# A two-layer convolution kernel on one core: kernel table by complex products, `u` stored from GpSimd, a variance product between the halves of an encoding

## The chip, the cores and the metric

The kernel runs on one core of a Trainium2 chip. The metric is the device time of one execution in microseconds (us). Three runs of the kernel before took 12704.01, 12707.76 and 12716.35 us, with the median 12707.76 us. One further execution was taken with the hardware profiler; every duration below is from that one.

Engines are named as the profile names them: PE is TensorE (matmuls; PEld is its weight loads), DVE is VectorE, ACT is ScalarE, POOL is GpSimd and SP is SyncE, which here only issues transfers. A name with a q (SPq, ACTq) is an engine's issue of a transfer.

## What is computed

The input `x` has 32 images of 128 channels by 32 x 32 pixels, in float32. Two layers run one after the other, each added to its input; the change touches only the beginning of the first:

```python
x = x + _L0_conv_ref(_gn(x), ...)     # group norm, then the layer below

h = jnp.einsum('bdl,de->ble', u, W_enc) + b_enc      # u: [32, 128, 1024], 1024 outputs
dtA = A * dt[:, None]                                # A: [1024, 4], complex
Bd = (jnp.exp(dtA) - 1.0) / A
vand = jnp.exp(dtA[:, :, None] * t)                  # t = 0 .. 63
K = 2.0 * jnp.einsum('dn,dnl->dl', Cc * Bd, vand).real   # a causal filter of 64 taps per output
y = irfft(rfft(z) * rfft(K))[..., :L]                # z = h transposed: each row filtered with K
y = gelu(y + D[:, None] * z);  g = y @ W_glu + b_glu
...                                                  # gate, layer norm, decoding
# second layer: group norm, then a deformable convolution of 64 taps
```

The group norm `_gn` has 32 groups of 4 channels; it subtracts the mean of a group and divides by the square root of its variance.

## The kernel before

The program has four parts in a row: `ssm_kernel_table` (L42), `ssm_convolution` (L186), `main_block` (L590) and `deformable_redo` (L1342). The first runs beside the beginning of the second.

**The table.** `ssm_kernel_table` makes the 64 filter taps of all 1024 outputs. The outputs lie on 128 partitions by 8 chunks, with 4 complex modes each, so `KN` is 32. From the small [128, 32] arrays `re`, `im` (the real and imaginary part of dtA), `cbr` and `cbi` (of 2 C B) it makes [128, 32, 64] arrays: `e` = exp(re t) (L142, L143), the angle im t (L144), its sine and its cosine less one (`sincos`, L64 to L78: six DVE operations, two sines on ACT, one more on DVE), and then (cos cbr - sin cbi) e (L146 to L149). The sum over the 4 modes goes into `kp` (L155 to L158), and SP stores `kp` to `kp_d` (L159). A scheduler orders these operations among the first ones of the next part.

**The first encoding.** `ssm_convolution` goes through 8 chunks of 128 outputs: `encode(k)` and then `convolve(k, z)`. For k > 0, `encode` loads the normalised images `u` from `u_d` and multiplies them. For k = 0 it makes them: a loop over t = 0 .. 34 (L264) in which several images are under way, each by a generator `group_norm_steps` (L162) of five steps:

1. L169, ACT: copy of `xt` into `u` with the sum per channel;
2. L172, PE: the product with `gavg`, which gives the group mean;
3. L174 and L175, ACT: the negative mean, and the sum of squares about it (the elementwise result goes to `u` and is overwritten later);
4. L178, PE: the product for the variance;
5. L180 on ACT (square root), L181 and L182 on DVE (reciprocal, and `u` = (xt - mean) / deviation).

Iteration t does, in the order of the program: step 5 of image t-2; the store of that `u` to `u_d`, issued by ACT (L267); step 3 of image t-1; the load of `xt` of image t, issued by SP (L272), and step 1 of it; `image(t-3)`; step 4 of image t-1; step 2 of image t. `image(b, u)` (L232) multiplies the eight 128-pixel blocks of `u` with the encoding weights, four into each of two PSUM banks (L237, eight matmuls that the profile shows as 16 passes), and then two DVE operations (L242) add the bias and write `z[0]` and `z[1]`. This order is kept on every engine (`manual_schedule`), and each engine takes its own instructions strictly one after the other.

Buffers: `u` has 5, `xt` has 6 (tag `yo`), the small group norm values have 4. PSUM has 4 buffers of two banks, which the two small products of an image and its encoding take in turn. `z[1]` lies where the table's arrays were, and its first write waits for the store of `kp`.

**What follows.** `convolve` loads filter matrices `toe` from `kp_d` (SP, L302), multiplies (L320), and stores `y_d` from POOL (L357). `main_block` takes the bulk of the time. The change does not alter these parts.

Of the kernel before, what the change touches and what calls it, by code (L numbers as in the profile page):

```python
# [8 lines left out]
F32 = mybir.dt.float32  # L9
AF = mybir.ActivationFunctionType  # L10
ALU = mybir.AluOpType
# [4 lines left out]
P = 128  # L16
# [5 lines left out]
NT = 64  # L22
# [19 lines left out]
def ssm_kernel_table(nc, tc, ins, kp_d):  # L42

    KN = KD * N2
    with tc.tile_pool(name="ssm", bufs=1) as sp:
# [6 lines left out]
        def small(tag, shape=(P, KN)):  # L52
            return sp.tile(list(shape), F32, tag=tag, name=tag)
# [7 lines left out]
        tt = sp.tile([P, NT], F32, tag="tt", name="tt")  # L61
        nc.sync.dma_start(tt, ins["steps"].to_broadcast([P, NT]))

        def sincos(theta, shape, tag):  # L64

            k = small(f"{tag}_k", shape)
            r = small(f"{tag}_r", shape)
            nc.vector.tensor_scalar(k, theta, INV_2PI, MAGIC, op0=ALU.mult, op1=ALU.add)
            nc.vector.tensor_scalar(k, k, MAGIC, None, op0=ALU.subtract)
            nc.vector.scalar_tensor_tensor(r, k, -PI2_A, theta, op0=ALU.mult, op1=ALU.add)  # L70
            nc.vector.scalar_tensor_tensor(r, k, -PI2_B, r, op0=ALU.mult, op1=ALU.add)
            nc.vector.scalar_tensor_tensor(r, k, -PI2_C, r, op0=ALU.mult, op1=ALU.add)
            nc.vector.tensor_scalar(r, r, PI_MAX, -PI_MAX, op0=ALU.min, op1=ALU.max)
            s = small(f"{tag}_s", shape)
            nc.scalar.activation(s, r, AF.Sin)
            nc.scalar.activation(k, r, AF.Sin, scale=0.5)
            nc.vector.scalar_tensor_tensor(r, k, -2.0, k, op0=ALU.mult, op1=ALU.mult)
            return s, r  # L78
# [45 lines left out]
        cbr, cbi = small("cbr"), small("cbi")  # L124
# [7 lines left out]
        nc.vector.tensor_scalar_mul(cbi, cbi, 2.0)  # L132


        big = (P, KN, NT)
        e, ang = small("e", big), small("ang", big)
        t_b = tt[:, None, :].to_broadcast([P, KN, NT])

        def over_t(a):
            return a[:, :, None].to_broadcast([P, KN, NT])  # L140

        nc.vector.tensor_mul(e, over_t(re), t_b)  # L142
        nc.scalar.activation(e, e, AF.Exp)  # L143
        nc.vector.tensor_mul(ang, over_t(im), t_b)  # L144
        sv, cv = sincos(ang, big, "v")
        nc.vector.scalar_tensor_tensor(cv, cv, 1.0, over_t(cbr), op0=ALU.add, op1=ALU.mult)  # L146
        nc.vector.tensor_mul(sv, sv, over_t(cbi))
        nc.vector.tensor_sub(cv, cv, sv)
        nc.vector.tensor_mul(cv, cv, e)  # L149

        kp = sp.tile([P, KD, KPW], F32, tag="kp", name="kp")
        nc.gpsimd.memset(kp, 0.0)
# [9 lines left out]
def group_norm_steps(nc, pool, pm, gavg, eps, xt, out):  # L162


    s = pool.tile([P, 1], F32, tag="gn_s", name="gn_s")
    nm = pool.tile([P, 1], F32, tag="gn_m", name="gn_m")
    ss = pool.tile([P, 1], F32, tag="gn_ss", name="gn_ss")
    r = pool.tile([P, 1], F32, tag="gn_r", name="gn_r")
    nc.scalar.activation(out, xt, AF.Identity, accum_out=s)  # L169
    yield  # L170
    p = pm(0)
    nc.tensor.matmul(p, gavg, s, start=True, stop=True)  # L172
    yield
    nc.scalar.mul(nm, p, -1.0)  # L174
    nc.scalar.activation(out, xt, AF.Square, bias=nm, accum_out=ss)  # L175
    yield
    p = pm(1)
    nc.tensor.matmul(p, gavg, ss, start=True, stop=True)  # L178
    yield
    nc.scalar.activation(r, p, AF.Sqrt, bias=eps)  # L180
    nc.vector.reciprocal(r, r)  # L181
    nc.vector.tensor_scalar(out, xt, nm, r, op0=ALU.add, op1=ALU.mult)  # L182
    yield


def ssm_convolution(nc, tc, const, ins, x, u_d, kp_d, y_d):  # L186
# [12 lines left out]
    with tc.tile_pool(name="cvt", bufs=3) as tp, tc.tile_pool(  # L199
        name="cvz", bufs=1  # L200
    ) as zp, tc.tile_pool(name="cv1", bufs=1) as one, tc.tile_pool(
        name="cvu", bufs=5
    ) as up, tc.tile_pool(name="cvy", bufs=6) as yp, tc.tile_pool(
        name="cvg", bufs=4
    ) as gp, tc.tile_pool(name="cv_ps", bufs=4, space=PSUM) as psum:

        def banks(name):
            return psum.tile([P, 2, 512], F32, tag="ps", name=name)
# [11 lines left out]
        def block(g, j):  # L220

            return 2 * ORDER[j] + g

        def encode(k):

            z = [
                pool.tile([P, P // 2, NB, B, 2], F32, tag=f"z{g}", name=f"z_{k}_{g}")
                for g, pool in enumerate((one, zp))
            ]
            bias = b_enc[:, k * P : (k + 1) * P]  # L230

            def image(b, u):  # L232
                both = banks(f"psz_{k}_{b}").rearrange("p g (j d) -> p g j d", j=NB)
                for g in range(2):
                    for j in range(NB):
                        lo = block(g, j) * P
                        nc.tensor.matmul(  # L237
                            both[:, g, j, :], u[:, lo : lo + P], w_enc[:, k * P : (k + 1) * P],
                            start=True, stop=True,
                        )  # L240
                for g in range(2):
                    nc.vector.tensor_add(  # L242
                        z[g][:, :, :, b, :].rearrange("p d j e -> p j d e"),
                        both[:, g].rearrange("p j (d e) -> p j d e", e=2),
                        bias.rearrange("p (d e) -> p d e", e=2)[:, None].to_broadcast(
                            [P, NB, P // 2, 2]
                        ),
                    )

            if k > 0:  # L250
                for b in range(B):
                    u = up.tile([P, L], F32, tag="u", name=f"u_{k}_{b}")
                    nc.sync.dma_start(u, u_d[b])
                    image(b, u)
                return z


            running = {}

            def step(b):  # L260
                if b in running:
                    next(running[b][1])

            for t in range(B + 3):  # L264
                step(t - 2)
                if t - 2 in running:
                    nc.scalar.dma_start(u_d[t - 2], running[t - 2][0])  # L267
                step(t - 1)
                if t < B:
                    u = up.tile([P, L], F32, tag="u", name=f"u_{k}_{t}")  # L270
                    xt = yp.tile([P, L], F32, tag="yo", name=f"xt_{t}")
                    nc.sync.dma_start(xt, x[t])  # L272

                    def pm(n, t=t):
                        return banks(f"gn_ps_{t}_{n}")[:, 0, 0:1]

                    running[t] = u, group_norm_steps(
                        nc, gp, pm, const["gavg"], const["eps"], xt, u
                    )
                    step(t)  # L280
                if t >= 3:
                    image(t - 3, running.pop(t - 3)[0])
                step(t - 1)
                step(t)
            return z

# [82 lines left out]
        with tc.manual_schedule():  # L369
            for k in range(KD):  # L370
                convolve(k, encode(k))
# [1002 lines left out]
@with_exitstack  # L1374
def kernel(ctx: ExitStack, tc: tile.TileContext, ins, out):
    nc = tc.nc
    x = ins["x"]
    cpool = ctx.enter_context(tc.tile_pool(name="const", bufs=1))
    dram = ctx.enter_context(tc.tile_pool(name="scratch", bufs=1, space=DRAM))

    const = {}
    for name in ("gavg", "davg"):
        const[name] = cpool.tile([P, P], F32, tag=name, name=name)
        nc.sync.dma_start(const[name], ins[name])
    const["eps"] = cpool.tile([P, 1], F32, tag="eps", name="eps")
    nc.vector.memset(const["eps"], 1e-5)
    const["one"] = cpool.tile([P, 1], F32, tag="one", name="one")
    nc.vector.memset(const["one"], 1.0)
    offmax = cpool.tile([P, B], F32, tag="offmax", name="offmax")

    kp_d = dram.tile([D, KPW], F32, tag="kp_d", name="kp_d")
    u_d = dram.tile([B, C, L], F32, tag="u_d", name="u_d")
    y_d = dram.tile([D, B, NJ, P], F32, tag="y_d", name="y_d")
    x1_d = dram.tile([B, C, L], F32, tag="x1_d", name="x1_d")

    ssm_kernel_table(nc, tc, ins, kp_d)
    ssm_convolution(nc, tc, const, ins, x, u_d, kp_d, y_d)
    main_block(nc, tc, const, ins, x, u_d, y_d, x1_d, out, offmax)
    deformable_redo(nc, tc, const, ins, x1_d, out, offmax)
# [85 lines left out]
```

## Time and profile before

| | |
|---|---|
| median of three runs | 12707.76 us |
| the profiled execution, its own time | 12713.35 us |
| its span, from the first to the last instruction | 12711.4 us |
| mean granted PE clock | 0.973 |
| busy: PE, DVE, ACT, POOL | 96%, 61%, 43%, 71% of the span |
| 60 to 180 us (most of the first encoding): granted PE clock | 0.77 |
| the same stretch: PE, DVE, ACT, POOL busy | 92.2, 60.3, 68.8, 0 us of 120 |
| the same stretch: DMA share, and bytes moved | 0.67, 225 GB/s |
| first matmul of `convolve(0)` (L320) | at 181.48 us |

A row of the timeline reads: start and duration in us, engine, line, operation, result <- operands, sizes, count, and in brackets how long the engine had been idle and what ended that. In a table of stretches the columns are the stretch, its length, the busy time (and number) of PE, PEld, DVE, ACT and POOL, the granted PE clock as a share of full speed, the busy share of the DMA engines, and GB/s. In a list of waits they are the total in us, the number of times and the longest.

### The profile page before, as it was taken

To read this page: it belongs to the slowest core of one execution; us is meant where nothing else is said; L and a number is where in the kernel's file an instruction comes from. 1 tells how busy PE (TensorE), PEld (TensorE's weight loads), DVE (VectorE), ACT (ScalarE), POOL (GpSimd) and SP (SyncE) were. 2 spreads that over 40 slices of the span, in tenths; PEclk is the share of its full clock that TensorE was granted. 3 is DMA by queue.
4 is the path that set the end of the run, shared out by engine and by line. 5 is a ranking of instruction groups with operands and counts; after the bars stand their busy time and mean duration, and the time that the engine had idled before them with its cause. 6 is when DMAs were issued, how large, how long until landed. Compare 5 with 4: busy or idle time off the path is not lost.

```text
span 12711.4 us, 162031 instructions
## 1 busy us (share of the span) xinstructions
PE 12198.8 (96%) x51362; PEld 6670.1 (52%) x51362; DVE 7803.7 (61%) x14315; ACT 5485.8 (43%) x7823; POOL 8975.3 (71%) x11691
## 2 busy tenths in 40 slices
PE   7999899999999999999999999999999999999965
PEld 7999444444444444444444444444444444444444
DVE  5555126666666666666666666666666666666666
ACT  4344124444444444444444444444444444444443
POOL 2455127777777777777777777777777777777779
PEclk9999999999999999999999999999999999999976
DMA  7899236666766666667666676666666667667666
GB/s 237 266 277 277 74 82 181 180 183 186 188 179 179 177 177 188 181 177 186 179 185 180 185 188 180 178 176 177 188 180 182 184 179 186 181 181 188 180 183 182
DMA packets 1521951, 2350.46 MB, mean 185 GB/s; under 512 B 619586, under 2 KB 835266, under 8 KB 1520066
## 3 DMA queue, kind: packets, MB, share of 16 engines
q1 hardware_dynamic: 1382210, 2027.97, 60.4%
q10 hardware_dynamic: 89728, 177.76, 3.8%
q0 software_dynamic: 49152, 134.28, 3.5%
q8 instruction: 413, 6.77, 0.2%
q14 instruction: 448, 3.67, 0.1%
HBM read 2016.61 MB, written 407.02 MB: 191 GB/s over the span
## 4 chain that ended last, share of the span: by engine, by line
PE 81%; DMA 6%; POOL 5%; DVE 3%; SPq 2%; issue 2%; ACT 1%; ACTq 0%; DVEq 0%; POOLq 0%
PE gpv L837 25%; PE gpg L814 24%; PE dps L1233 16%; PE psy L320 5%; PE gph L853 3%; PE psz L237 3%; DMA ds<-dhat 3%; PE gpo L742 3%; POOL prod L1276 3%; POOL do L1295 1%; DMA dhy<-rel_d 1%; POOL gs L738 1%; SPq L1131 1%; DVE ds L1157 1%; DVE prod L1249 1%
## 5 line engine op out<-in xcount | busy, mean ns | idle before, releaser
L1276 POOL TENSOR_TENSOR prod<-prod 128x256 f32<-128x256 f32 (+3 forms) x7616 | 5797.4, 801 | 1112.8 <-DVE prod L1249 1112.8
L1249 DVE TENSOR_TENSOR prod<-dps,k_weight_slots 128x512 f32<-128x512 f32 (+16 forms) x8704 | 3124.2, 407 | 1615.3 <-PE dps L1233 1204.5
L814 PE MATMUL gpg<-gy,g_w_glu 128*128 128x512 f32 x8192 | 3759.6, 602 | 41.0 <-ACT gs L821 26.9
L837 PE MATMUL gpv<-gy,g_w_glu 128*128 128x512 f32 x8192 | 3739.8, 599 | 0.0
L1233 PE MATMUL dps<-ds,dxw 64*128 64x128 f32 (+14 forms) x23936 | 2753.9, 374 | 262.5 <-DVE prod L1249 229.6
L1157 DVE TENSOR_TENSOR ds<-ds,dhy 128x640 f32<-128x640 f32 (+2 forms) x2176 | 2363.9, 1127 | 784.5 <-ACT dhy L1152 426.9
L1233 PEld LDWEIGHTS dps<-ds,dxw 64*128 64x128 f32 x23936 | 1968.0, 196 | 1343.1 <-issue 432.0
L814 PEld LDWEIGHTS gpg<-gy,g_w_glu 128*128 128x128 f32 x8192 | 1519.9, 191 | 1963.2 <-issue 1907.1
L837 PEld LDWEIGHTS gpv<-gy,g_w_glu 128*128 128x128 f32 x8192 | 1509.7, 190 | 1878.6 <-issue 1878.6
L738 POOL TENSOR_TENSOR gs<-gs,gq 128x256 f32<-128x256 f32 x896 | 751.5, 859 | 1856.7 <-ACT gq L874 1856.7
L1151 ACT ACTIVATE dhy<-dhy,k_minus_y 128x640 f32<-128x640 f32 (+2 forms) x2176 | 1698.5, 781 | 483.4 <-DMA dhy<-rel_d 174.0
L1152 ACT ACTIVATE dhy<-dhy,one 128x640 f32<-128x640 f32 (+2 forms) x2176 | 1726.5, 793 | 71.1
L874 ACT ACTIVATE gq<-gr 128x512 f32<-128x512 f32 x448 | 281.3, 628 | 2557.7 <-DVE gr L866 2551.8
L845 DVE SCALAR_TENSOR_TENSOR gs<-gpv,k_b_glu,gs 128x512 f32<-128x512 f32 x512 | 383.9, 750 | 1357.8 <-PE gpv L837 1289.4
L821 ACT ACTIVATE gs<-gpg,k_b_glu 128x512 f32<-128x512 f32 x512 | 351.3, 686 | 1860.7 <-PE gpg L814 1846.8
L357 POOL DMA_DIRECT2D y_d<-yo x1024 | 590.0, 583 | 693.5 <-ACT yo L344 633.5
L1284 POOL TENSOR_TENSOR dacc<-dacc,prod 128x256 f32<-128x256 f32 (+6 forms) x1184 | 886.7, 749 | 55.2
L738 POOL TENSOR_TENSOR gs<-gs,gr 128x256 f32<-128x256 f32 x896 | 810.7, 925 | 0.0
L320 PE MATMUL psy<-toe,z 128*128 128x192 f32 x4096 | 668.0, 326 | 7.4 <-DVE z L242 5.5
L320 PEld LDWEIGHTS psy<-toe,z 128*128 128x128 f32 x4096 | 663.0, 196 | 11.7 <-DVE z L242 6.8
L335 DVE TENSOR_TENSOR psy<-psy,t 128x256 f32<-128x256 f32 (+2 forms) x768 | 333.7, 434 | 346.1 <-ACT t L328 329.3
L853 PE MATMUL gph<-gu,k_W_enc 128*128 128x512 f32 x1024 | 530.2, 600 | 0.4 <-DVE gs L845 0.4
(164 smaller groups left out, 6055.0 us busy)
## 6 DMA issues: line engine op xcount, KB each, us to landing
dhy<-rel_d SPq DMA_DIRECT2D x3264, 160.0 KB
ds<-dhat SPq DMA_DIRECT2D x832, 400.0 KB
ds<-dhat SPq DMA_DIRECT2D x448, 480.0 KB
dxw<-dxw_d SPq DMA_DIRECT2D x832, 224.0 KB
y_d<-yo POOLq DMA_DIRECT2D x1024, 128.0 KB, 4.2
gy<-y_d SPq DMA_DIRECT2D x512, 256.0 KB
u<-u_d SPq DMA_DIRECT2D x224, 512.0 KB
dhat<-dh ACTq DMA_DIRECT2D x256, 390.0 KB
```

Of the source, the lines that this page charges most:

```text
L320: nc.tensor.matmul(ps[:, c // 2, c % 2, :], rows[i][:, (g * CG + c0 + c) // 2, c % 2, :], toe[:, c0 + c, :], start=True, stop=True,)
L738: nc.gpsimd.tensor_add(to[:, cut], to[:, cut], more[:, cut])
L814: nc.tensor.matmul(gate, w_glu[:, k, D + m * P : D + m * P + P], ys[k], start=(k == 0), stop=(k == KD - 1),)
L837: nc.tensor.matmul(val, w_glu[:, k, m * P : m * P + P], ys[k], start=(k == 0), stop=(k == KD - 1),)
L853: nc.tensor.matmul(h, w_enc[:, m * P : (m + 1) * P], u, start=True, stop=True)
L1151: nc.scalar.activation(t, t, AF.Abs, bias=minus_y)
L1152: nc.scalar.activation(t, t, AF.Relu, scale=-1.0, bias=const["one"])
L1157: nc.vector.tensor_mul(s_of[h][:, cut], s_of[h][:, cut], t)
L1233: nc.tensor.matmul(to[side][:, :, :, r0:r1], xw[half, w, :], frm, start=True, stop=True,)
L1249: nc.vector.tensor_mul(bass.AP(tensor=at_y.tensor, offset=at_y.offset, ap=[at_y.ap[0], [H, m], [step * (KS - 1) + skew, rows], [1, run],], ...
L1276: nc.gpsimd.tensor_add(row(to, lo, hi), row(to, lo, hi), row(frm, lo, hi))
L1284: nc.gpsimd.tensor_add(to, to, total[:, slot * H : (slot + nj) * H].rearrange("p (s y) -> p s y", y=H),)
```

## The change

Three edits, all in the first 182 us of the program:

1. **The table.** Exponential, sine and cosine are made for 16 values of t instead of 64: the eight multiples of 8 (the far steps, 8a) and 0 to 7 (the near steps, b). The near ones are multiplied with the complex constants (`w`), and the 64 taps are made as the real part of the product of near and far: two [128, 32, 8, 8] products and their difference.
2. **The store of `u`** to `u_d` is issued by POOL instead of ACT.
3. **Step 4 of image t-1**, the product for its variance, is issued on PE between the two halves of `image(t-3)`: after the four matmuls into the first bank and before the other four. For t < 3, with no `image`, it stays where it was.

Apart from this the order of the built program is the same on all engines. New line numbers are larger by 20 from L151 to L240 and by 22 or 23 after that: L169 becomes L189, L174 L194, L178 L198, L180 L200, L182 L202, L237 L257, L242 L264, L267 L289.

```diff
-        big = (P, KN, NT)
-        e, ang = small("e", big), small("ang", big)
-        t_b = tt[:, None, :].to_broadcast([P, KN, NT])
+        few = (P, KN, 16)
+        t16 = sp.tile([P, 16], F32, tag="t16", name="t16")
+        nc.vector.tensor_copy(t16[:, 0:8], tt[:, 7::8])
+        nc.vector.tensor_copy(t16[:, 8:16], tt[:, NT - 8 : NT])
+        e, ang = small("e", few), small("ang", few)
+        t_b = t16[:, None, :].to_broadcast([P, KN, 16])
...
-        sv, cv = sincos(ang, big, "v")
-        nc.vector.scalar_tensor_tensor(cv, cv, 1.0, over_t(cbr), op0=ALU.add, op1=ALU.mult)
-        nc.vector.tensor_mul(sv, sv, over_t(cbi))
-        nc.vector.tensor_sub(cv, cv, sv)
-        nc.vector.tensor_mul(cv, cv, e)
+        sv, cv = sincos(ang, few, "v")
+        nc.vector.scalar_tensor_tensor(cv, cv, 1.0, e, op0=ALU.add, op1=ALU.mult)
+        nc.vector.tensor_mul(sv, sv, e)
+        w = [small(f"w{i}", (P, KN, 8)) for i in range(3)]
+        near = cv[:, :, 8:], sv[:, :, 8:]
+        nc.vector.tensor_mul(w[0], near[0], over_t(cbr, 8))
+        nc.vector.tensor_mul(w[2], near[1], over_t(cbi, 8))
+        nc.vector.tensor_sub(w[0], w[0], w[2])
+        nc.vector.tensor_mul(w[1], near[0], over_t(cbi, 8))
+        nc.vector.tensor_mul(w[2], near[1], over_t(cbr, 8))
+        nc.vector.tensor_add(w[1], w[1], w[2])
+        parts = []
+        for i, far in enumerate((cv, sv)):
+            o = small(f"o{i}", (P, KN, 8, 8))
+            nc.vector.tensor_mul(
+                o,
+                w[i][:, :, None, :].to_broadcast([P, KN, 8, 8]),
+                far[:, :, :8, None].to_broadcast([P, KN, 8, 8]),
+            )
+            parts.append(o.rearrange("p n a b -> p n (a b)"))
+        cv = parts[0]
+        nc.vector.tensor_sub(cv, cv, parts[1])
...
-            def image(b, u):
+            def image(b, u, between=None):
...
+                    if g == 0 and between is not None:
+                        between()
...
-                    nc.scalar.dma_start(u_d[t - 2], running[t - 2][0])
+                    nc.gpsimd.dma_start(u_d[t - 2], running[t - 2][0])
...
-                    image(t - 3, running.pop(t - 3)[0])
-                step(t - 1)
+                    image(t - 3, running.pop(t - 3)[0], between=lambda: step(t - 1))
+                else:
+                    step(t - 1)
```

More of the change, by code (lines that the diff above doesn't have):

```diff
@@ L132, in ssm_kernel_table, with over_t @@
         nc.vector.tensor_scalar_mul(cbi, cbi, 2.0)
-        big = (P, KN, NT)
-        e, ang = small("e", big), small("ang", big)
-        t_b = tt[:, None, :].to_broadcast([P, KN, NT])
-        def over_t(a):
-            return a[:, :, None].to_broadcast([P, KN, NT])
+        few = (P, KN, 16)
[4 more added lines that the diff above has]
+        t_b = t16[:, None, :].to_broadcast([P, KN, 16])
+        def over_t(a, n=16):
+            return a[:, :, None].to_broadcast([P, KN, n])
         nc.vector.tensor_mul(e, over_t(re), t_b)
```

## The prediction

> **What bounds it now.** I read the page's chain first: it is PE for 81% of the span, in parts that the change leaves alone. Every edit lies before the first L320, at 181.48 us. As the order of the rest is untouched, the question is by how much that matmul comes earlier, and whether the gain is kept. It should be kept: from there PE is full (the stretch 200 to 220 us shows PE busy 20.00 of 20.00), and what L320 needs is there long before (the `toe` loads are issued from 152 us on).
>
> Then the timeline of one image of the first encoding, at full clock:
>
> ```profile
> 62.88 0.17 ACT L174 ACTIVATE gn_m<-gn_ps 128x1 f32<-128x1 f32 x1 [1.47 <-DVE u L182]
> 63.08 1.15 ACT L175 ACTIVATE u<-xt,gn_m 128x1024 f32<-128x1024 f32 x1
> ...
> 64.23 1.04 ACT L169 ACTIVATE u<-xt 128x1024 f32<-128x1024 f32 x1
> ...
> 64.38 0.38 PE L178 MATMUL gn_ps<-gn_ss,gavg 128*128 128x1 f32 x2 [0.79 <-ACT u L175]
> ...
> 65.27 0.24 ACT L180 ACTIVATE gn_r<-gn_ps,eps 128x1 f32<-128x1 f32 x1
> 65.42 0.38 PE L172 MATMUL gn_ps<-gn_s,gavg 128*128 128x1 f32 x2 [0.66 <-ACT u L169]
> ...
> 65.66 2.03 PE L237 MATMUL psz<-w_enc,u 128*128 128x128 f32 x16
> 65.74 0.81 DVE L182 TENSOR_SCALAR u<-xt,gn_m,gn_r 128x1024 f32<-128x1024 f32 x1
> 66.58 0.35 ACTq L267 DMA_DIRECT2D u_d<-u  x1
> 66.98 0.17 ACT L174 ACTIVATE gn_m<-gn_ps 128x1 f32<-128x1 f32 x1 [1.47 <-DVE u L182]
> ```
>
> The image takes 4.10 us, a loop through ACT: 2.63 us of its own (62.88 to the end of L180), then 1.47 idle, because the store of `u` stands next in ACT's queue and waits for L182. No engine is full. The clock differs between stretches:
>
> ```profile
> 77.40:80.80 3.40, 2.73 (x23) 2.47 (x21) 2.81 (x6) 1.00 (x5) 0.00 (x0) 0.98 0.45 175
> 80.80:84.20 3.40, 1.62 (x13) 1.53 (x14) 1.63 (x4) 2.26 (x5) 0.00 (x0) 1.00 0.96 304
> 84.20:87.60 3.40, 2.83 (x15) 2.45 (x13) 1.62 (x4) 2.60 (x6) 0.00 (x0) 0.53 0.76 251
> 87.60:91.00 3.40, 3.40 (x17) 3.40 (x17) 0.60 (x1) 2.34 (x5) 0.00 (x0) 0.50 0.58 204
> ```
>
> PE busy 80% of a stretch keeps the full clock, 48% is followed by half clock, and only a stretch of 100% ends that. At half clock the 16 passes take 3.76 us, L178 (queued behind them) comes late, and one image in three takes about 5.3 us. From L182 of image 2 (48.13) to that of image 31 (177.73) it is 129.6 us for 29 images: 4.47 us each.
>
> The head, from the waits after 40 us and the timeline:
>
> ```profile
> DVE z L242 <- DMA kp_d<-kp: 5.6, 1, 5.6
> ```
>
> DVE makes the table until 41.8 us, then its queue stands behind the first write of `z[1]` until `kp` has landed; L182 of image 2 follows.
>
> **Part 1, the table.** DVE is what ends it. Removed, on 128x2048: ten operations of 2.29 us (L142, L144, L70, L71, L72, L77, L146 to L149) and three of 1.21 (L68, L69, L73): 26.5 us. Added: eight of 128x512 at 0.68 (the row of L155), 5.4; three TENSOR_SCALAR of 128x512, between 0.17 (128x32) and 1.21, nearest a quarter of the latter plus start-up, 0.4 each, 1.2; two copies at 0.2; six products of 128x256 at 0.43 (L335's row), 2.6; three of 128x2048 at 2.29, 6.9. Sum 16.5, so 10.0 us less. ACT's three functions shrink from 1.91 to some 0.6 us each, but the sines stand behind L189 of image 0, whose `xt` lands at 13.1 us: 13.1 + 1.23 + a table load of 1.28 = 15.7, and sines until 16.9, where DVE has its own work until about 15.5. That wait costs up to 1 us; more overlap of small operations may give as much. The store of `kp` lands 5.4 us after issue as before, with the same two loads and two stores of `u` near it. **Head: 10.0 us earlier (8.5 to 11).**
>
> **Parts 2 and 3, the loop.** ACT now passes from L200 to L194 without the wait for L202 and the issue. What remains is a ring through PE, per image at full clock:
> - L192 to L194: 0.41 (0.38, and 0.03 to start, as at 14.35 to 14.97 with the slow product's 0.59);
> - L194 to L198: 1.49 (62.88 to 64.37: L174, L175 and its accumulator);
> - L198 to the second half: 0.24 (as 65.42 to 65.66);
> - half of the 16 passes, then L192 of the next image: 1.02.
>
> Sum 3.16 us. L189 would allow L192 earlier, 2.53 after L194 (62.88 to 65.41) against 2.75. Part 3 adds a wait: the second half, and L192 behind it, stand behind L198, which waits for ACT's L195 while PE idles 1.49 + 0.41 - 0.24 - 1.02 = 0.64 us; this is inside the ring. Without part 3 the passes would run through, L198 would start 0.24 + 2.03 after L192 and still be done before ACT wants it, and the ring would be L192 to L194 and on to L189: 0.41 + 2.53 = 2.94. So at full clock part 3 by itself costs 0.2 us per image, some 6 us, if nothing else holds the loop; at half clock PE is full either way. DVE needs 0.1 + 0.85 for L201 and L202 and 1.29 for the pair L264, 2.3 of 3.16. PSUM's ring holds: L198 takes the bank that the previous pair frees at about 4.1 us after its L194, and is due at 3.16 + 1.49.
>
> Transfers: each image loads 524 KB and stores 524 KB. From 60 to 180 us, 225 GB/s went at a share of 0.67, so 336 at full share, or 3.12 us per image; the stretch at 0.96 (304 GB/s) gives 3.3. Ring and transfers are nearly equal, and two such limits don't overlap perfectly. I take **3.25 us** (bounds 3.1 and 3.4).
>
> The store on POOL: POOL is idle until 192 us.
>
> ```profile
> 192.12 4.82 POOL L357 DMA_DIRECT2D y_d<-yo  x8 [185.06 <-ACT yo L344]
> DMA to landing us min/median/max: 2.4/4.2/7.8
> ```
>
> It issues 32 rows of 4 KB in 0.58 us; 128 rows are not in the trace: between 0.58 and 4 x 0.58 = 2.33, under 3.25 either way. The landing matters through the 5 buffers of `u`: L189 of image t waits for the store of image t-5. L202 ends about 1.9 us after its iteration's L194 (behind the pair L264), L189 starts 1.35 after the L194 three iterations on, so the store has 3 x 3.25 - 0.55 = 9.2 us. The bounds for its landing are 2.4 and 4 x 4.2 = 16.8; the nearest estimate is 4.2 and 2.2 more for 393 KB more at half of 350 GB/s: 6.4, and up to 8.2 with a slow issue. It is hidden, with 1 to 3 us to spare. ACT's issue (0.35) goes; SP's queue keeps its order.
>
> **Sum.** Head -10.0; 29 x (4.47 - 3.25) = -35.4; image 2 still at half clock after the `kp` wait, 4.4 instead of 3.25 (at half clock each product holds PE for 0.45, 73.61 to 74.07, and the 16 passes for 3.5), +1.2. Total **-44.2 us**. On the profiled 12713.35 this is 12669.1; the median of the runs is 5.6 lower, so 12663.5.
>
> **Rivals.**
> - **The clock keeps alternating.** PE is busy 2.51 of 3.16 (79%) or of 3.4 (74%). In this loop full clock followed stretches of 74 to 80%, and was lost after about 40 to 58%; but near the end of the program (12358, 12532 and 12560 us) stretches of 70 to 78% lost it, with other matmuls. If it drops for two stretches in four, as now, 6.8 us at 3.25 and 6.8 at 4.4 make 3.65 images in 13.65: 3.74 each. 29 x 0.73 = 21.2, with the head 31: **12677**. The Trainium skill ("TensorE: Matmul & The Clock Gate", Part 1, "What's actually happening") lets the clock fall only after an idle window of about 3.4 us; by that the loop would never lose it, before or after, and this rival would have no chance. The trace disagrees: the longest gap there is about 1.8 us and the clock falls to 0.50. I go by the rows.
> - **The loop gains almost nothing.** The clock stays low (4.4 per image, PE full; against it: full stretches ended it each time), or the store lands in 12 to 13 us so that `u` holds the loop. Gain 12: **12696**.
> - **Slower.** A store from POOL lands in proportion to its bytes: 16.8 us. Then 3P - 0.55 = 16.8, P = 5.8, 29 x 1.3 = 38 lost against 10 won: **12736**. It turns to a loss from P = 4.82, a landing of 13.9 us. For it: no store of this size from POOL is in the trace, and 7.8 occurred for a quarter of it. Against it: those 4.2 are at a DMA share of 0.99, here 0.67. The Trainium skill ("DMA: Bandwidth & Descriptors", "SWDGE vs HWDGE vs iDMA") speaks against the change: DVE in its two-port mode locks GpSimd out of the descriptor rings. No run here shows it; L202 holds DVE 0.81 us per image, which leaves the spare time above.
>
> **Chances.** Forecast 0.56 (12655 to 12671), alternating clock 0.23, little gain 0.14, slower 0.07. What a measurement can tell from no change is about 0.2%, 25 us: faster means below 12682, which the first two give: 0.79; same 0.14; slower 0.07. Range: from the ring alone at its best (P 3.1, head 11: 50 us, and 4 us for the scatter of a median) 12654, up to the little gain, 12692.
>
> **What the profile after would show.** `kp` stored near 31.6 us instead of 41.84, L202 of image 2 near 38; then 3.1 to 3.4 us from L194 to L194, ACT idle about 0.6 per image <-PE L192, none <-DVE u L202; PE idle 0.6 before L198 <-ACT L195; granted clock near 1.0 from 50 to 130 us; first L343 near 137 us. It is wrong if ACT's L189 waits for `u_d`, if POOL's issue takes over 3 us, if the clock shows 0.5 stretches, or if L257 waits for L202.

## The result, and the profile after

The kernel after takes 12680.04 us (median of 8 runs, 12657.99 to 12686.34), the kernel before, run beside it, 12712.08 (8 runs, 12698.83 to 12717.96). The ratio is 0.9973 with a 95% interval of 0.9962 to 0.9984, so **32 us less** (20 to 48), where 44 were forecast. The profiled execution took 12680.48 us, its span 12678.8; for before it was 12713.35 and 12711.4.

The timeline of one image of the first encoding after the change, from L192 to the next L192. Columns: start, busy time, engine, line, operation, and in brackets the idle time ahead of it and what ended it:

```profile
62.69 0.28 PE L192 MATMUL gn_ps<-gn_s,gavg 128*128 128x1 f32 x2
...
63.00 0.17 ACT L194 ACTIVATE gn_m<-gn_ps 128x1 f32<-128x1 f32 x1 [0.40 <-PE gn_ps L192]
...
64.28 0.81 DVE L202 TENSOR_SCALAR u<-xt,gn_m,gn_r 128x1024 f32<-128x1024 f32 x1
...
64.50 0.38 PE L198 MATMUL gn_ps<-gn_ss,gavg 128*128 128x1 f32 x2 [0.54 <-ACT u L195]
...
64.75 1.14 PE L257 MATMUL psz<-w_enc,u 128*128 128x128 f32 x8
...
65.39 0.53 POOL L289 DMA_DIRECT2D u_d<-u  x1 [2.50 <-DVE u L202]
...
65.72 0.28 PE L192 MATMUL gn_ps<-gn_s,gavg 128*128 128x1 f32 x2
...
66.04 0.17 ACT L194 ACTIVATE gn_m<-gn_ps 128x1 f32<-128x1 f32 x1 [0.40 <-PE gn_ps L192]
```

The image takes 3.03 us instead of 4.10. ACT no longer waits 1.47 us for DVE's L182; its only gap is 0.40, for PE's product L192. PE waits 0.54 ahead of L198 for ACT's L195. These are the two waits of the ring that the prediction drew. L202 ends at 65.09, and it is POOL that stands there waiting for it, with nothing behind.

The same four stretches as before (columns: us, busy time and count of PE, PEld, DVE, ACT, POOL, then the granted clock, the DMA share and GB/s):

```profile
77.40:80.80 3.40, 2.86 (x26) 2.67 (x25) 2.17 (x4) 2.96 (x9) 0.77 (x2) 1.00 0.98 359
80.80:84.20 3.40, 2.87 (x26) 2.67 (x25) 2.24 (x5) 2.61 (x7) 0.82 (x2) 1.00 1.01 370
84.20:87.60 3.40, 2.87 (x25) 2.67 (x25) 2.54 (x5) 2.89 (x8) 0.53 (x1) 1.00 1.03 341
87.60:91.00 3.40, 2.87 (x26) 2.67 (x24) 2.54 (x6) 2.97 (x7) 0.53 (x1) 1.00 1.00 343
```

PE is busy 84% of every stretch and keeps the full clock where two of four had 0.50. The DMA share, 0.45 to 0.96 before, is now 0.98 to 1.03: whether that is now the limit is a question of its own.

The store of `u`, from the view of that tensor in the first 125 us, and the wait for `kp` from the list of waits in the first 60:

```profile
L289 POOL DMA_DIRECT2D u_d<-u x30: 531/531/772, 26.0 to 123.0; - x30
...
DMA to landing us min/median/max: 5.2/6.4/7.7
```

```profile
DVE z L264 <- DMA kp_d<-kp: 6.9, 1, 6.9
```

POOL issues 128 rows in 0.53 us, and they land in 6.4. `kp` is stored at 31.47 us instead of 41.84, but DVE waits 6.9 us for its landing where it waited 5.6; L202 of image 2 starts at 39.13 instead of 48.13.

The first L343 (L320 before) starts at 131.91 us instead of 181.48: **49.6 us earlier**. The first store of `out` comes 48.8 us earlier (2173.6 and 2222.4), the last only 32.3 (12670.8 and 12703.0). So the first part won more than forecast, and 16.6 us are gone in the long part behind it, in which the order of all instructions is the same. That is what the experiments had to explain, beside the parts' own worth.

### The profile page after: what moved, and what is told of

It reads as the page before. It is cut to its first block, busy times and chain, and to the rows that moved or that the text cites. A ratio compares the mean times of both kernels' runs of the same rounds, so it can differ in the third digit from the quotient of the medians.

```text
span 12678.8 us, 162092 instructions
## 1 busy us (share of the span) xinstructions
PE 12184.7 (96%) x51362; PEld 6648.1 (52%) x51362; DVE 7769.1 (61%) x14324; ACT 5480.7 (43%) x7822; POOL 8987.0 (71%) x11723
## 4 chain that ended last, share of the span: by engine, by line
PE 82%; DMA 7%; POOL 5%; DVE 2%; SPq 2%; issue 2%; ACT 1%; ACTq 0%; DVEq 0%; POOLq 0%
PE gpv L860 25%; PE gpg L837 24%; PE dps L1256 17%; PE psy L343 5%; PE psz L257 3%; PE gph L876 3%; PE gpo L765 3%; DMA ds<-dhat 3%; POOL prod L1299 2%; DMA dhy<-rel_d 1%; POOL do L1318 1%; SPq L1154 1%; POOL gs L761 1%; DVE ds L1180 1%; DMA dxw<-dxw_d 1%
## 5 line engine op out<-in xcount | busy, mean ns | idle before, releaser
L1180 DVE TENSOR_TENSOR ds<-ds,dhy 128x640 f32<-128x640 f32 (+2 forms) x2176 | 2340.9, 1116 | 791.7 <-ACT dhy L1175 431.9
L343 PE MATMUL psy<-toe,z 128*128 128x192 f32 x4096 | 670.9, 327 | 7.5 <-DVE z L264 5.5
L343 PEld LDWEIGHTS psy<-toe,z 128*128 128x128 f32 x4096 | 663.0, 196 | 14.7 <-DVE z L264 6.8
```

The lines of the kernel that those rows point to most:

```text
L343: nc.tensor.matmul(ps[:, c // 2, c % 2, :], rows[i][:, (g * CG + c0 + c) // 2, c % 2, :], toe[:, c0 + c, :], start=True, stop=True,)
L1180: nc.vector.tensor_mul(s_of[h][:, cut], s_of[h][:, cut], t)
```

## The experiments

Two theories of the 16.6 us. *Scatter*: the long part takes a different time in each execution, whatever stands ahead of it. *Given back*: the change makes it longer. And three questions on the loop: what part 3 costs, whether the DMA or the ring holds the 3.03 us, and whether the wait for `kp` can go. The runs fall into four groups, each with runs of before beside it: the comparison above is A; B, C and D follow, and the kernels of each of these three ran on one chip.

### Group B: both kernels once more, and two parts alone

`again_before` and `again_after` are the two kernels without an edit.

> The kernel before, unchanged, a second time. In the first two traces the stretch from the first store of `out` to the last takes 10480.6 us before and 10497.2 us after, so 16.6 of the 49.6 us that the first L343 won are gone there, although the instructions and their order are the same. Theory `scatter`: the length of this stretch varies by 10 to 20 us between executions of one program, because DVE and POOL hold each other up in an order that small shifts tip; then this run's stretch is not 10480.6 but anything from 10465 to 10510, and the times of the runs of one kernel spread over some 20 us. Theory `given back`: the change itself makes the stretch longer; then this run gives 10480.6 within 3 us.

> The kernel after, unchanged, a second time. First L343 at 131.9 us within 1 us by both theories. `Given back`: the stretch between the first and the last store of `out` is 10497 within 3 us again, and the median over all runs stays 32 us (within 5) under that of before. `Scatter`: the stretch is anything from 10465 to 10510, the drift against the kernel before goes up and down at other places than in the first trace, and the difference of the medians moves from 32 towards the 44 to 50 us that the first part wins.

Before took 12751.1 us here (21 runs), and 12753.86 as `again_before` (11 runs, 12726.17 to 12768.36); `again_after` 12698.16 (5 runs, 12692.95 to 12717.05), ratio 0.9964 (0.9951 to 0.9978), **53 us less** (28 to 62). The stretch from first to last store of `out` took 10520.1 us in the kernel before and 10512.4 in the kernel after: not 10481 and 10497, and now it is the kernel after that is shorter. First L343 stood at 131.61, and L320 of `again_before` at 180.84. *Given back* has fallen as it was put down (10480.6 and 10497, each within 3 us): what was lost in the first pair of traces came the other way in the second, and the 11 runs of `again_before` are 42 us apart.

`table_alone` is before with part 1 only.

> Part 1 alone (the table by products; store of `u` on ACT and the order of the matmuls as before). If the parts add: `kp` is stored near 31.5 us, L202 of image 2 near 39, the loop stays at 4.1 us per image at full clock and 4.4 to 4.5 in the mean, first matmul of the convolution near 172.5 us (181.48 before), 9 us less in the total, 12703 beside 12712. If the 5.4 to 6.9 us landing of `kp` is set by what else is under way, the head gains 9 to 10.5. The stretch between the stores of `out`: 10481 by `given back` if the store or the order of the matmuls is to blame, 10497 if the table is; anything from 10465 to 10510 by `scatter`.

`kp` was stored at 30.39, L202 of image 2 stood at 36.89, and the first matmul of the convolution at 170.51: 11.0 us earlier than in before, 10.3 than in `again_before`. In time it is 12744.67 (11 runs) beside 12751.1, ratio 0.9993 (0.9984 to 1.0002): 6 us less, which the interval doesn't tell from none. So the table by itself wins more (11.2 at L202) than the 9.0 of the full change.

`store_alone` is before with part 2 only:

```diff
-                    nc.scalar.dma_start(u_d[t - 2], running[t - 2][0])
+                    nc.gpsimd.dma_start(u_d[t - 2], running[t - 2][0])
```

> Part 2 alone (store of `u` issued by GpSimd; the old table, variance product behind the whole encoding). The head stays: L202 of image 2 near 48. The loop: by my ring, 0.41 + 2.53 = 2.94 us per image at full clock, if nothing else holds it; if the DMA (524 KB in and 524 KB out at 344 to 348 GB/s) is the limit, 3.03 as with part 3. First matmul of the convolution at 48.1 + 92.8 = 140.9 us for 3.03, 138.3 for 2.94. If the clock falls again without part 3, 3.7 per image and 160 us. Total 41 us under before, 12671, by `scatter` with 10 us either way; 12688 if the store causes the loss in the long part.

It gave the loop 2.96 us per image, with the clock up, and the first matmul at 137.77, 43.1 us earlier than in `again_before`. The time is 12709.25, ratio 0.9964 (0.9951 to 0.9978): 42 us less, as expected, from this one line.

### Group C: part 3 taken away and taken alone, fewer transfers, `kp` kept

Before took 12827.0 us here (10 runs).

`no_between` is after without part 3:

```diff
-                    image(t - 3, running.pop(t - 3)[0], between=lambda: step(t - 1))
-                else:
-                    step(t - 1)
+                    image(t - 3, running.pop(t - 3)[0])
+                step(t - 1)
```

> Parts 1 and 2 without part 3 (the variance product stands behind the whole encoding of the image). With part 3 the loop takes 3.05 to 3.06 us per image from L202 of image 2 to that of image 31 (88.4 and 88.9 us for 29), and part 2 alone, on the old table, took 85.56 for 29, 2.95. If part 3 costs what I worked out at full clock, the ring here is 2.94 to 2.95, the first matmul of the convolution comes 3 us earlier than with part 3, and it isn't the DMA that held 3.05. If the DMA holds the loop, or the clock drops without part 3, 3.05 or more. Head: if it is the matmuls between that made `kp` late (31.5, where part 1 alone stored it at 30.4), it goes at 30.4 here and L202 of image 2 stands near 37; if it is the store on GpSimd, 31.5 and 39. Total: 0 to 5 us under after by this, which the long part's scatter (medians 44 to 53 us under before) hides.

The loop took 2.96 us per image, 0.07 less than with part 3; `kp` was stored at 31.52 and L202 of image 2 stood at 39.11, as in after. The first matmul came at 128.60, 3.3 us earlier than in after. The time is 12771.38, ratio 0.9958 (0.9944 to 0.9971), 56 us under before. So part 3 costs the change some 3 us. The lists of waits of after (40 to 130 us) and of `no_between` (40 to 127) show, one under the other, which wait PE has once per image:

```profile
PE gn_ps L198 <- ACT u L195: 13.9, 26, 0.5
```

```profile
PE gn_ps L192 <- ACT u L189: 14.1, 25, 0.6
```

Without part 3 the loop runs through ACT's L189, as the prediction had drawn it (2.94). It isn't part 3 that made `kp` late: with ACT free of its wait the images come sooner, and in after L201, L202 and L264 of images 0 and 1 stand between the last additions of the table on DVE.

`between_alone` is before with part 3 only (the first and last hunks of the change behind the table).

> Part 3 alone (old table, store of `u` on ACT). Theory of the prediction: the loop through ACT (2.63 of its own and 1.47 of waiting for L182) isn't touched at full clock, 4.10 us; but at half clock, where the variance product stood behind all 16 slow passes and one image in three took 5.3 us, it now stands behind 8 of them, 1.9 us sooner, so that all images take about 4.1: 29 x 0.37 = 11 us, L182 of image 31 near 167 instead of 177. Rival: at half clock PE is full either way and nothing is won: 4.4 to 4.47 and 177. A second rival: the product in the middle waits for ACT with the second half behind it, as it costs 0.1 us per image at full clock: 4.2 there. `kp` is issued at 41.8 as before.

All three expectations fell: it is **51 us slower**, 12878.47, ratio 1.0040 (1.0026 to 1.0053), and its first matmul of the convolution stands at 242.57, 61 us later than in before. The timeline of one image:

```profile
69.34 0.17 ACT L174 ACTIVATE gn_m<-gn_ps 128x1 f32<-128x1 f32 x1 [4.04 <-DVE u L182]
...
70.84 0.38 PE L178 MATMUL gn_ps<-gn_ss,gavg 128*128 128x1 f32 x2 [2.39 <-ACT u L175]
...
71.08 1.82 PE L237 MATMUL psz<-w_enc,u 128*128 128x128 f32 x8
...
72.94 1.29 DVE L244 TENSOR_TENSOR z<-psz,b_enc 128x512 f32<-128x512 f32 x2 [4.02 <-PE psz L237]
...
74.33 0.81 DVE L182 TENSOR_SCALAR u<-xt,gn_m,gn_r 128x1024 f32<-128x1024 f32 x1
75.18 0.35 ACTq L269 DMA_DIRECT2D u_d<-u  x1
75.57 0.17 ACT L174 ACTIVATE gn_m<-gn_ps 128x1 f32<-128x1 f32 x1 [3.60 <-DVE u L182]
```

Read it as one chain: ACT's L174 and L175 release PE's L178; behind it come the second half of the passes; behind these DVE's L244; behind that, on DVE, L182 of the image; for L182 the store waits on ACT, and behind the store the next L174. Part 3 has closed a ring through three engines, 6.23 us here and 6.67 in most images. PE then has too little to do:

```profile
80.00:100.00 20.00, 13.91 (x62) 13.03 (x61) 6.51 (x12) 7.79 (x18) 0.00 (x0) 0.50 0.51 157
```

The clock stands at 0.50 from 78 to 146 us and from 157 to 239. In the full change the same L202 stands behind the same pair, but no queue waits for it except POOL's: part 2 is what makes part 3 bearable. (The full change has the new table as well, but the table is done long before these images.)

`half_store` is after with the stores of every other image's `u` left out; the later passes load the stored neighbour:

```diff
-                if t - 2 in running:
+                if t - 2 in running and t % 2 == 0:
...
-                nc.sync.dma_start(u, u_d[b])
+                nc.sync.dma_start(u, u_d[b - b % 2])
```

> After, but `u` of every other image alone is stored, and later passes load the stored neighbour in place of those left out: the work is the same, the stores of the first encoding are halved, 16 x 524 KB less. DMA stands at a share of 1.00 in this loop (344 to 348 GB/s). If the DMA holds the loop at 3.05 us, it now falls towards what the ring needs without it, 2.9 or less, and the first L343 comes 4 us or more earlier. If the ring through PE and ACT holds it, the loop stays at 3.03 to 3.06 with the DMA share near 0.75, and the share of 1.00 was load that fills the gaps and holds nobody up.

The loop stayed at 3.03 us, with a DMA share of 0.82 where 0.75 was expected; the time is 12778.07, 49 us under before. Two stretches of it, and below them the same of `no_between`, which moves all bytes:

```profile
60.00:80.00 20.00, 16.79 (x138) 15.65 (x138) 14.00 (x26) 16.95 (x41) 1.60 (x3) 1.00 0.82 266
80.00:100.00 20.00, 16.25 (x132) 14.92 (x131) 14.59 (x28) 17.39 (x39) 1.59 (x3) 1.00 0.82 273
```

```profile
60.00:80.00 20.00, 16.05 (x136) 15.46 (x135) 14.53 (x27) 17.53 (x42) 3.73 (x7) 1.00 0.99 357
80.00:100.00 20.00, 16.32 (x138) 15.73 (x137) 14.50 (x28) 17.82 (x40) 3.74 (x7) 1.00 1.00 354
```

A quarter of the bytes less changes nothing in the loop, and `no_between` moves more bytes per us than after at the same share of 1.00. So the ring through ACT and PE holds the loop, and a share of 1.00 says that the DMA engines have something under way all the time, not that somebody waits for it. What it does change is the head: DVE waits 5.4 us for `kp` here, about as before the change (5.6), and 6.9 in after; L202 of image 2 stands at 37.72 and the first L343 at 130.22, 1.7 us earlier than in after. So the images' transfers beside `kp` are what made its landing longer.

`kp_kept` gives `kp` memory of its own, which `z[1]` doesn't reuse:

```diff
-        kp = sp.tile([P, KD, KPW], F32, tag="kp", name="kp")
+        kp = keep.tile([P, KD, KPW], F32, tag="kp", name="kp")
...
+    with tc.tile_pool(name="keep", bufs=1) as keep:
+        ssm_kernel_table(nc, tc, ins, kp_d, keep)
+        ssm_convolution(nc, tc, const, ins, x, u_d, kp_d, y_d)
```

> After, but `kp` lies in memory of its own that stays until the convolution is done, so the first write of `z[1]` (6.94 us of waiting in after) has nothing to wait for. L202 of image 2 comes near 32 to 33 instead of 39.1. If the ring holds the loop from there, everything behind is 6 to 7 us earlier: first L343 near 125.5 instead of 131.9. Rival: the transfers of the first images then hold the loop (33.5 MB at 346 GB/s are 97 us, and loads begin near 10 us), and half of it or less is won: 128 to 131.

L202 of image 2 came at 32.35 and the first L343 at 127.13: 4.8 us won, between the two. Images 6 to 9 took 3.7 to 4.3 us, from L194 to L194. In the timeline of ACT and the view of `u_d` (first 125 us):

```profile
41.64 1.06 ACT L189 ACTIVATE u<-xt 128x1024 f32<-128x1024 f32 x1 [0.85 <-DMA u_d<-u]
```

```profile
DMA to landing us min/median/max: 2.9/6.6/9.9
```

Stores take up to 9.9 us to land, and L189 waits for one twice (0.85 and 0.88 us): the prediction's room for a landing was 9.2. These waits fall in the first two of the four long images; the other two ran at half clock (0.50 from 47.6 to 54.4 us). The time is 12772.04, ratio 0.9956 (0.9942 to 0.9969).

### Group D: the first part by itself, after a third time, and the best version

Before took 12841.62 us here (9 runs). `cut_before` and `cut_after` leave out all that stands behind the convolution and fill `out` from the first 128 channels of `y_d`.

> The kernel before, with everything behind the convolution left out (both layers' rest, which takes some 11.4 ms); in its place `out` is filled with the first 128 channels of the convolution's result. What the change moves is all in what is left, so its time shows the first part's gain without the long part's scatter. Between 1300 and 1450 us, runs within 3 us of each other.

> The kernel after, cut in the same way. If the 49.6 us by which the first L343 comes earlier are real and lasting up to the end of the convolution, it is 48 to 51 us under the cut kernel before, run for run. If part of the gain is lost in the convolution, where the loads of the table stand behind the loop's transfers, it is 44 or less.

1388.81 us (4 runs, 1387.69 to 1390.06) and 1337.02 (4 runs, 1336.69 to 1337.19): **51.8 us less**, just above the 48 to 51 that were expected, with runs 2.4 and 0.5 us apart. The two profiled executions are 50.6 us apart (1387.69 and 1337.05), and 49.4 of these are there at the first matmul of the convolution (181.25 and 131.82). Nothing is lost up to its end.

> The kernel after once more, on another chip or at another time, for the gain in the whole program. Medians so far: 32 us under before (interval 14 to 48), then 53 (28 to 62). `Scatter`: the gain is the 49 to 50 us of the first part plus or minus some 15 us of the long part, so 35 to 65 here. `Given back` would need 32 again. The stretch from first to last store of `out` was 10520, 10512, 10521 and 10525 us in four kernels on one chip and 10580 to 10584 in four on another; so within 12 us of what other kernels have on the same chip.

12799.47, ratio 0.9965 (0.9952 to 0.9979): 42 us less (27 to 62). (The interval of the first comparison, 14 to 48 in this text, should read 20 to 48.) The stretch between the stores of `out` was 10618.7 us, 21.7 more than in `best` on the same chip, where 12 at most were expected.

`best` is `no_between` with `kp` kept and six buffers of `u` (`bufs=6` in the pool `cvu`).

> Parts 1 and 2 without part 3, `kp` in memory of its own, and 6 buffers of `u` in place of 5. Without part 3 the loop is 2.96 us per image, not 3.03; with `kp` kept L202 of image 2 stood at 32.35 and images 6 to 9 took 3.7 to 4.3, two of them because ACT's L189 waited 0.9 us for a store of `u` that took 9.9 us to land. If the sixth buffer ends these waits, L202 of image 31 comes near 32.4 + 29 x 2.96 + 1 to 2 for the half clock near 47 us, 119 to 120, and the first matmul of the convolution near 123 to 124 (131.9 in after): 8 us less. If the transfers of the first images (DMA share 1.03 to 1.05 from 35 to 50 us) hold it all the same, 126 and 5 to 6 us less. In the whole program this is within the scatter: 55 to 60 us under before at the middle.

The loop ran at 2.96 us from image 5 to the end, at full clock throughout and without a wait for a store. Stores issued between 30 and 60 us landed in 5.3 to 10.6 us, 9.0 at the median; by the prediction's sum the room with five buffers is 3 x 2.96 - 0.55 = 8.3, so that they would have felt it. The first matmul came at 120.28 us, 3 us better than expected: no half clock came, for which 1 to 2 us were put in, and the first three steps from L202 to L202 after image 2 took 7.2 us, less than three of 2.96. The time is 12775.99 (5 runs, 12758.87 to 12782.52), ratio 0.9944 (0.9931 to 0.9958): 66 us under before, and 23 under the median of `third_after` on the same chip, of which 12 are at the first matmul. It beats both kernels.

### The long part

From the store times and the trace's records of the granted clock: the stretch from first to last store of `out` in the twelve whole profiles, and how much of it stood at half clock.

| group | kernel | stretch, us | at half clock, us |
|---|---|---|---|
| A | before, after | 10480.6, 10497.2 | 539, 558 |
| B | again_before, again_after | 10520.1, 10512.4 | 592, 559 |
| B | table_alone, store_alone | 10520.6, 10525.0 | 554, 601 |
| C | no_between, between_alone | 10581.5, 10580.3 | 660, 645 |
| C | half_store, kp_kept | 10583.6, 10582.4 | 672, 654 |
| D | third_after, best | 10618.7, 10597.0 | 714, 651 |

Within a group the kernels differ by 3 to 22 us, in no order of the change; between groups, by up to 138. The length goes with the time at half clock (correlation 0.97 over the twelve), at some 0.77 us for each us of it. That is a correlation: a longer stretch with more idle time of PE could be why the clock falls, and a lower clock could be why the stretch is longer, and no run here parts the two. I first thought that DVE and POOL hold each other up in main_block (single L1180, L1157 before, of up to 5.98 us). There are 3 to 10 of over 3 us in a profile, and they don't go with the length: `between_alone` has 3 and `no_between` 10, at 10580 and 10582. What makes the long part slower in one group than in another, the chip or the time, stays open.

## Why the prediction was right, and where it was not

- **Direction and size.** Forecast 44.2 us less; measured 32, 53 and 42, each interval holding 44 (20 to 48, 28 to 62, 27 to 62). The first part alone gives 51.8. So the size was some 5 to 7 us short where it can be measured to a microsecond or two (49.6 and 51.8), and right within what the whole program shows. That is partly luck: in the first comparison the first part won 5 us more than forecast and the long part took 16.6 back. Its 12680 even lies outside the 12655 to 12671 of the forecast and nearest the 12677 of the alternating clock; only the rows of the trace tell the two apart. (The upper end of the range, 12692, isn't the 12696 of the little gain that it names.)
- **Head, forecast -10.0, came out at -9.0.** The step that failed is "lands 5.4 us after issue as before, with the same two loads and two stores of `u` near it": the wait was 6.9. The images' transfers beside `kp` are the reason: `half_store`, with fewer of them, waits 5.4 (the DMA share from 30 to 35 us is 0.94 in after, 0.86 in `half_store` and 0.75 in `table_alone`). That `kp` was stored at 31.47, forecast 31.6, is two deviations that cancel: part 1 alone stored it at 30.39, 1.2 us earlier than forecast, and in the full change DVE's work for images 0 and 1 stands ahead of it and gives 1.1 back.
- **Loop, forecast 3.25, came out at 3.03.** This is the mis-sized term: 29 x 0.22 = 6.4 us. The ring's path and its waits were right. Its pieces in the image shown are 0.31 (forecast 0.41), 1.50 (1.49), 0.25 (0.24) and 0.97 (1.02), together 3.03 beside 3.16. That is 0.13 of the 0.22, and most of it is PE's product L192, taken at 0.38 and 0.28 in the rows. The other 0.09 is the step from 3.16 to 3.25, "two such limits don't overlap perfectly": the transfers were no limit. The 336 GB/s came from dividing a rate by a share; `no_between` moves 357.
- **Image 2 at half clock, forecast +1.2, came out at +1.0**: from L202 of image 2 to that of image 31 it is 88.86 us, 29 x 3.03 = 87.87.
- **Part 3 costs, forecast 0.2 us per image "if nothing else holds the loop".** It does cost, 0.07, because the ring with it is shorter than worked out (3.03); without it, 2.96 against a forecast of 2.94. That it would lose 51 us on the old kernel the expectation ahead of that run didn't see, though the pieces were all named.
- **The store on POOL.** Issue 0.53 (bounds 0.58 and 2.33: below both), landing 6.4 median, the estimate; the slower rival needed 13.9, and the little gain 12 to 13. So `u` never held the loop in after.
- **The alternating clock** (chance 0.23) didn't come: PE was 0.84 busy, and the clock kept 1.00. What spoke for it was in part misread. The clock's records change only at steps of 3.41 us. In before, in the stretches of 3.41 us that end at the falls near 12358.7, 12532.8 and 12560.1 us, PE was busy 1.78, 2.22 and 1.96 us, which is 52 to 65% and not the 70 to 78% of the prediction; from 40 us on no fall in that profile follows a stretch of over 69%, in after none of over 66%. The Trainium skill's rule ("TensorE: Matmul & The Clock Gate", Part 1, "What's actually happening"), by which only an idle window lowers the clock, would give this too; but in `between_alone` the clock fell to 0.50 near 71, 78, 150 and 157 us, and from 60 us to the end of its loop no idle time of PE is over 2.43 us (in before 1.92, where the prediction has about 1.8), so the rows speak against it again.
- **"It should be kept".** It is kept to the end of the convolution, as the two cut kernels show. In the whole program the three comparisons have a mean of 42; if each has the interval given, that of the mean is some 33 to 52. It holds the 49.6 of the first matmul, and it also leaves room for a loss of up to some 16 us in the long part, so that the rest is not shown. In the first pair of profiles the gain seemed not to be kept: two single profiles, compared 10,000 us behind the edit, can differ by 10 to 20 us where the code is the same (the table above).

## What to carry to other kernels

When an in-order queue's next item is a DMA that waits for another engine, moving that one issue to an engine with nothing behind it can be worth more than any work saved; here one line gave 42 us, and the table's 10 us of DVE work gave 6 to 11. Draw the ring of waits for each edit alone as well as for all together: the reordered product costs 0.07 us an image with the store on POOL, and 2.1 with it on ACT. And measure a head's gain where it ends, with the rest cut away: the 51.8 us stood there within 3, while runs of one kernel of the whole program were 8 to 42 us apart.

## What the runs showed of the hardware

- POOL's issue of a store of 512 KB (128 rows of 4 KB) took 0.53 us, no more than the 0.58 of a store of a quarter of the bytes (L357 before: 32 rows of 4 KB, which go to `y_d` in 256 pieces of 512 bytes). So it isn't in proportion to rows or bytes; with what it does go, two shapes don't show.
- One core's loads and stores together moved 354 to 357 GB/s over 60 us of `no_between`, and 415 from 40 to 45 us in `kp_kept`; the prediction had 336 as the full share.
- The landing of a store differs with what else is under way, for the same bytes: 5.2 to 7.7 us in after, and 5.3 to 10.6 in `best` between 30 and 60 us, where up to 419 GB/s moved at a share of 1.03.
- The granted clock in these traces is 0.50 or 1.00 and nothing between, in pieces that are nearly all multiples of 3.41 us. This agrees with the Trainium skill ("TensorE: Matmul & The Clock Gate", Part 1, "What's actually happening"), which has a free-running window of 3413 ns and says that runs of one kernel differ by where it falls. Whether that is behind the scatter of the long part, no run here shows.
- The kernel before had medians of 12712, 12751, 12827 and 12842 us in the four groups: only kernels of one group are to be compared.

Not tried: the store of `u` from SP's queue, where the load of a later image would stand behind it.
